# Layer 3's sum over states by accumulating transposes, gates laid out by tokens, softplus summed by transfers, and GpSimd's quarter of B in 14 of 16 states

## The chip, the cores and the metric

The kernel runs on one core of one Trainium2 chip. The metric is the device time of one execution in microseconds (us), as a median of several executions. Names used below: PE is TensorE (its weight loads are listed apart, as PEld), DVE is VectorE, ACT is ScalarE, POOL is GpSimd, SP is SyncE, which here only issues transfers.

## What is computed

Four residual layers are applied one after the other to x, of shape 4 x 256 x 64 x 64; each layer first normalizes x over groups of 8 channels. Layer 0 is a deformable convolution, layer 1 attention over the 4096 pixels, layer 2 a second deformable operator. The change lies in layer 3, a selective state space layer (Mamba) over the L = 4096 pixels as tokens, with 512 inner channels and 16 states:

```python
xz = jnp.einsum('bld,ed->ble', xs, in_proj_w)
u, res = jnp.split(xz, 2, axis=-1)
u_t = lax.conv_general_dilated(u_t, conv_w, ...)          # causal, 4 taps, each channel alone
u = jax.nn.silu(u_t.transpose(0, 2, 1) + conv_b)
dbc = jnp.einsum('bld,ed->ble', u, x_proj_w)
dt, Bm, Cm = jnp.split(dbc, [DT_RANK, DT_RANK + D_STATE], axis=-1)
delta = jax.nn.softplus(jnp.einsum('blr,dr->bld', dt, dt_proj_w) + dt_proj_b)
deltaA = jnp.exp(jnp.einsum('bld,dn->bldn', delta, A))
deltaBu = jnp.einsum('bld,bln,bld->bldn', delta, Bm, u)
def step(state, inp):
    dA, dBu, c_t = inp
    state = dA * state + dBu
    y = jnp.einsum('bdn,bn->bd', state, c_t)
    return (state, y)
...
y = jnp.moveaxis(ys, 0, 1) + u * D
y = y * jax.nn.silu(res)
out = jnp.einsum('ble,de->bld', y, out_proj_w)
```

## The kernel before

The four images are worked off one after the other, each through layers 0 to 3. All arithmetic of layer 3 that matters here is in fp32.

Layer 3 cuts the 4096 tokens into 8 chunks of 512 (C = 512, chunks numbered j) and walks over 8 x 16 states s, with j = s // 16 and n = s % 16. Channels lie on the 128 partitions, in four blocks dc of 128; a tile of "128 x 2048" is four blocks of 512 tokens. One iteration of the main loop does, for one state:

- `product` on DVE (L1594): h = du x B, where du = delta x u and B comes as a row broadcast to all partitions by a matmul on PE (`state`, tile bn, L1579). In the states listed in `helped`, DVE does three of the four blocks and POOL does the fourth (`quarter`, tile hq, L1586) from a row bs that a transfer has broadcast.
- `scan(dc)`, four times: ACT makes da = exp(delta x A) for one block into one of two PSUM banks (L1675), and DVE runs the recurrence over the 512 tokens (L1677). With two banks, the exp of block dc can start only when the scan of block dc - 2 is done.
- POOL keeps the last column as the carry for the next chunk (L1697), and multiplies h by C, broadcast by a transfer into cn (L1700).
- PE adds h into y, two states later (`add`, L1557): for each block, a matmul with the identity as weights and h as 512 moving columns, accumulating in one PSUM bank per block. State 0 also adds D x u with a diagonal weight (L1556).

`helped` holds the states 14, 15 and 0 to 5 of each chunk, but not states 14 and 15 of chunk 0. The transfers of cn and bs are issued on SP two states ahead (`ahead`, L1570).

The order of everything on PE, ACT, DVE and POOL is the program's order. Around the states, other work is put by hand into slots (state, half): half 0 comes after the second scan, half 1 after the fourth, half 2 after POOL's multiply. `front(j)` prepares chunk j during chunk j - 1: its steps count from state 11 of chunk j - 2 (step 0 is five states before chunk j - 1; for chunk 1 two). They are: normalized x, four projections to `up` (L1293), the convolution as four matmuls a block (L1333), silu at step 7 (state 2), the shares dt, B, C (L1360), then softplus. Softplus is written as relu(z) + ln(1 + exp(-|z|)), where POOL adds the parts: ACT makes |z| in du and relu(z) in delta (L1381, L1382, states 4 and 5), then du = exp(-|z|) (L1414, step 11, state 6), w = 1 + du (L1418, state 7), du = 1 - w (L1423, second half of state 8), w = ln w (L1426, state 9). POOL adds du, du and w to delta (L1429, after states 6, 9 and 11; the two du terms, exp(-|z|) and 1 - w, add up to the rounding loss of w), and makes du = delta x u after state 13 (L1430). In chunk 0, where chunk 1 is prepared, the same steps lie in states 8 to 13. Three casts (L1395 to L1403) and two small subtractions on POOL (L1397, L1401) split B into bf16 parts in between.

The gate `res` of chunk j is projected like u, block by block (`gate`, in states 9 and 10), with in_proj's columns as weights and x as moving data, and copied by ACT into sres[:, dc, :]. After all 16 states of a chunk, in state 2 of the next one, `gated` multiplies the four banks of y with silu(res) on DVE (L1646), and `close` projects the result with out_proj and adds x (L1449, L1453; two output tiles ot, in states 6 and 8), copies it out by ACT (L1457) and stores it. All these side works on PE share one PSUM bank (`bank`), so the next one starts when ACT has emptied it. The last chunk has no next chunk to prepare; its slots hold the building of the next image's table for layer 0 (`table`), which also sends 8 large transfers at a time through SP's queue.

Of the kernel before, what the change touches and what calls it, by code (L numbers as in the profile page):

```python
# [9 lines left out]
F32 = mybir.dt.float32  # L10
# [3 lines left out]
ALU = mybir.AluOpType  # L14
AX = mybir.AxisListType

P = 128
# [11 lines left out]
DS = 16  # L29
# [34 lines left out]
class Net:  # L64
# [1064 lines left out]
    def layer3(self, x, out, nxt, early):  # L1129
# [7 lines left out]
        nc, tc = self.nc, self.tc  # L1137
        C = 512
        NC, LEAD = N // C, 5
        with (  # L1140
# [7 lines left out]
            win, cw, al, dd = (early[n] for n in ("win", "cw", "al", "d"))  # L1148
            cb, xpw, dtw, dtb, wo = self.loads(pa, "l3b")
# [3 lines left out]
            diag = pa.tile([P, 4, P], F32, tag="diag", name="diag")  # L1153
# [16 lines left out]
            def bank():  # L1170
                return self.psum.tile([P, C], F32, tag="ps", name="front")
# [5 lines left out]
            def first():  # L1177
# [99 lines left out]

                state(0)
                c["gates"] = [spare() for _ in range(4)]
                for dc, pg in enumerate(c["gates"]):  # L1280
                    project(pg, xn, 4 + dc)

            def project(j, dc, to):
                c = chunks[j]

                def pe():
                    c["b"] = bank()
                    for ct in range(2):
                        nc.tensor.matmul(
                            c["b"], win[:, ct, bass.ts(dc, P)], c["xn"][:, ct, :], start=(ct == 0), stop=(ct == 1)  # L1290
                        )

                return pe, lambda: nc.scalar.copy(to(), c["b"])  # L1293

            def gate(j, dc):
                def to():
                    if dc == 0:
                        chunks[j]["sres"] = pb.tile([P, 4, C], F32, tag="sres", name="sres")
                    return chunks[j]["sres"][:, dc, :]

                return project(j, 4 + dc, to)

            def gate_silu(j):
                sres = chunks[j]["sres"]
# [2 lines left out]
            def front(j):  # L1307
# [117 lines left out]
                put(*at["c"], None, over)  # L1425
                put(*at["ln"], None, lambda: nc.scalar.activation(c["w"], c["w"], AF.Ln))  # L1426

                for step, part in zip(at["sums"], ("du", "du", "w")):
                    put(step, 2, None, lambda part=part: nc.gpsimd.tensor_add(c["delta"], c["delta"], c[part]))  # L1429
                put(at["sums"][3], 2, None, lambda: nc.gpsimd.tensor_mul(c["du"], c["delta"], c["u"]))  # L1430

                for dc in range(4):
# [5 lines left out]
            def close(j):  # L1438

                c = chunks[j]  # L1440
                last = j == NC - 1
                todo = []

                def project(ot):
                    def pe():
                        c["b"] = pda.tile([P, C], F32, tag="da", name="out") if last else bank()
                        c["z", ot] = c["b"]
                        for dc in range(4):
                            nc.tensor.matmul(  # L1449
                                c["b"], wo[:, dc, bass.ts(ot, P)], c["sres"][:, dc, :], start=(dc == 0), stop=False  # L1450
                            )
# [8 lines left out]
                    return pe, rest  # L1460

                for ot in range(2):
                    todo.append((6 + 2 * ot, 1, *project(ot)))
                if j < NC - 2:
                    todo.append((10, -1, None, lambda: fetch(j)))

                    todo.append((2 + DS, 0, None, lambda: count(j)))
                return todo
# [82 lines left out]
            def add(j, n, h, half):  # L1551
                c = chunks[j]
                for dc in (2 * half, 2 * half + 1):
                    if n == 0:
                        c["ys", dc] = py.tile([P, C], F32, tag="y", name="y")
                        nc.tensor.matmul(c["ys", dc], diag[:, dc, :], c["u"][:, dc, :], start=True, stop=False)  # L1556
                    nc.tensor.matmul(c["ys", dc], self.ident, h[:, dc, :], start=False, stop=(n == DS - 1))  # L1557


            hs, helped = {}, [s for s in range(NC * DS) if s % DS in (14, 15, 0, 1, 2, 3, 4, 5) and s // 2 != 7]  # L1560

            def ahead(s):

# [76 lines left out]
                    filled = filled or pe is not None  # L1640
                    rest()

            def gated(j):
                c = chunks[j]
                for dc in range(4):
                    nc.vector.tensor_mul(c["sres"][:, dc, :], c["ys", dc], c["sres"][:, dc, :])  # L1646

            with tc.manual_schedule(
                engines={
# [195 lines left out]
```

## Time and profile before

| | us |
|---|---|
| median of 4 executions | 9455.42 (9452.51 to 9462.64) |
| the profiled execution's own time | 9472.06 |
| its span, first to last instruction | 9470.3 |
| layer 3 of image 0, in that span | about 1480 to 2414 |

Busy time of each engine in the whole span: PE 8248.3 (87%), weight loads 4377.5 (46%), DVE 7355.9 (78%), ACT 4945.6 (52%), POOL 6967.6 (74%). The four images look alike: the page's 40 slices repeat a pattern of ten, of which the last four are layer 3. The costliest groups of layer 3, over all four images:

| line, engine | what | count | busy us | mean ns |
|---|---|---|---|---|
| L1700 POOL | h x cn, 128 x 2048 | 508 | 2300.9 | 4529 |
| L1677 DVE | scan, 128 x 512, input h | 1800 | 2174.3 | 1264 |
| L1675 ACT | exp to da, 128 x 512 | 2048 | 1395.9 | 689 |
| L1557 PE | y by the identity, 512 columns | 4096 | 1924.5 | 603 |
| L1594 DVE | product, 1536 or 2048 elements | 512 | 1025.1 | 2002 |

How to read it: an fp32 matmul leaves two records in the trace (4096 records of L1557 for 2048 matmuls), and the durations of PE's records overlap, so starts are compared instead. In a timeline, each line gives the start, the time, the engine, the line and the operation, with its shape, and how many instructions were merged; in brackets stands the idle time before it and what ended it. DVE's idle time in image 0's layer 3 is mostly put down to ACT's da: 10.0 us in 8 waits between 1505 and 2360.

### The profile page before, as it was taken

The numbers are of one execution on the slowest core, as the hardware profiler recorded it, in microseconds if no ns is written. First come the engines' busy times: TensorE is split into PE (matmuls) and PEld (weight loads), VectorE is DVE, ScalarE is ACT, GpSimd is POOL, SyncE is SP. The second block draws the span as 40 slices with busy tenths as digits, with TensorE's granted clock in tenths as the row PEclk, the third lists the DMA queues.
The fourth block names the chain that finished last, engine by engine and source line by source line (L and its number), as shares of the span: only waits on it lengthen the run. The fifth ranks groups of instructions, "written<-read, shape, count | busy, mean of one in ns | idle before, by whom it ended". The sixth has DMA issues, their size and how long they took to land. (4 is left out here: it accounts for less than half of the span.)

```text
span 9470.3 us, 94901 instructions
## 1 busy us (share of the span) xinstructions
PE 8248.3 (87%) x31767; PEld 4377.5 (46%) x31767; DVE 7355.9 (78%) x8241; ACT 4945.6 (52%) x7653; POOL 6967.6 (74%) x4164
## 2 busy tenths in 40 slices
PE   5789888998778988899877898889987789889997
PEld 3643464443464346344346434634434643563443
DVE  5764498999676449899967645999996764589998
ACT  4743335666574333666657433366665743336664
POOL 4746687998574668799856466879985746788997
PEclk9999999999999999999998999999999999999999
DMA  8840012222783001122378300122237820111221
GB/s 287 319 152 1 26 54 60 65 67 85 269 318 126 1 29 55 58 68 64 102 264 320 111 1 32 52 63 64 66 114 274 320 86 1 37 56 54 63 63 52
DMA packets 409189, 1017.75 MB, mean 107 GB/s; under 512 B 38833, under 2 KB 106834, under 8 KB 406642
## 3 DMA queue, kind: packets, MB, share of 16 engines
q0 software_dynamic: 165888, 604.05, 17.8%
q1 hardware_dynamic: 242802, 407.54, 14.1%
q8 instruction: 253, 4.15, 0.2%
q14 instruction: 246, 2.02, 0.1%
HBM read 849.60 MB, written 88.10 MB: 99 GB/s over the span
## 5 line engine op out<-in xcount | busy, mean ns | idle before, releaser
L1700 POOL TENSOR_TENSOR h<-h,cn 128x2048 f32<-128x2048 f32 x508 | 2300.9, 4529 | 41.3 <-POOL carry L1697 0.6
L1677 DVE TENSOR_TENSOR_SCAN h<-da,carry,h 128x512 f32<-128x512 f32 x1800 | 2174.3, 1264 | 82.1 <-ACT da L1675 33.9
L1675 ACT ACTIVATE da<-delta,l3a 128x512 f32<-128x512 f32 x2048 | 1395.9, 689 | 1208.3 <-DVE h L1677 1204.6
L1557 PE MATMUL y<-h,ident 128*128 128x512 f32 x4096 | 1924.5, 603 | 14.5 <-POOL h L1700 14.4
L371 POOL DMA_INDIRECT g<-tab,idx x1152 | 1361.9, 1182 | 706.4 <-DVE r L380 274.3
L592 POOL TENSOR_TENSOR acc<-acc,e 128x1024 f32<-128x1024 f32 x480 | 1125.9, 2346 | 540.3 <-ACT e L588 518.7
L415 PE MATMUL pz<-cols,l0w 128*128 128x256 f32 x4608 | 1218.9, 411 | 187.0 <-ACT cols L404 63.6
L1557 PEld LDWEIGHTS y<-h,ident 128*128 128x128 f32 x4096 | 788.7, 194 | 1063.0 <-issue 975.9
L380 DVE SCALAR_TENSOR_TENSOR r<-g,wx,r 128x512 f32<-128x512 f32 x1152 | 858.2, 745 | 372.7 <-ACT r L379 252.2
L489 DVE TENSOR_REDUCE m<-pm 128x3 f32<-128x1536 f32 (+2 forms) x340 | 599.5, 1763 | 700.2 <-PE pm L479 700.2
L415 PEld LDWEIGHTS pz<-cols,l0w 128*128 128x128 f32 x4608 | 898.9, 206 | 355.5 <-DVE cols L404 91.3
L588 ACT ACTIVATE e<-sc 128x1024 f32<-128x1024 f32 x512 | 496.1, 1020 | 1029.6 <-PE sc L575 1029.5
L1594 DVE TENSOR_TENSOR h<-du,bn 128x2048 f32<-128x2048 f32 (+1 forms) x512 | 1025.1, 2002 | 4.0 <-PE bn L1579 3.9
L599 PE MATMUL cx<-e,v 128*128 128x512 f32 x2048 | 1001.1, 616 | 0.0
L379 ACT ACTIVATE r<-g,wx 128x512 f32<-128x512 f32 x1152 | 826.4, 717 | 235.1 <-DMA g<-tab,idx 196.7
L882 DVE TENSOR_TENSOR prod<-ring,A 128x1280 f32<-128x1280 f32 (+1 forms) x640 | 783.6, 1266 | 67.3 <-DMA ring<-ring 37.0
L908 PE MATMUL pacc<-ident,prod 128*128 128x128 f32 x4864 | 631.8, 284 | 153.9 <-POOL prod L897 115.2
L908 PEld LDWEIGHTS pacc<-ident,prod 128*128 128x128 f32 x4864 | 555.4, 145 | 217.7 <-POOL prod L897 135.3
L397 PE MATMUL pt<-ident,acc 128*128 128x128 f32 x2304 | 428.6, 294 | 245.2 <-DVE acc L388 163.1
L599 PEld LDWEIGHTS cx<-e,v 128*128 128x128 f32 x2048 | 352.5, 189 | 599.4 <-issue 596.9
L387 ACT ACTIVATE acc<-r,wy 128x256 f32<-128x256 f32 x1152 | 571.5, 496 | 28.6 <-DVE r L380 25.8
L388 DVE SCALAR_TENSOR_TENSOR acc<-r,wy,acc 128x256 f32<-128x256 f32 x1152 | 548.6, 477 | 2.0 <-ACT acc L387 2.0
(271 smaller groups left out, 11452.9 us busy)
## 6 DMA issues: line engine op xcount, KB each, us to landing
cn<-cd SPq DMA_DIRECT2D x512, 256.0 KB
bs<-cd SPq DMA_DIRECT2D x248, 256.0 KB
tab<-vtnext SPq DMA_DIRECT2D x96, 512.0 KB
ring<-ring SPq DMA_DIRECT2D x288, 126.0 KB
ring<-ring SPq DMA_DIRECT2D x288, 124.0 KB
g<-tab,idx POOLq DMA_INDIRECT x1152
tab<-vt SPq DMA_DIRECT2D x28, 640.0 KB
x<-in_x SPq DMA_DIRECT2D x64, 256.0 KB
```

What stands on the lines that cost most here:

```text
L371: nc.gpsimd.indirect_dma_start(out=g[:], out_offset=None, in_=tab[:, :], in_offset=bass.IndirectOffsetOnAxis(ap=idx[:, t, k : k + 1], axis=0),
L379: nc.scalar.mul(r, g[:, :, 0, :], wx[:, 0, t, k : k + 1])
L380: nc.vector.scalar_tensor_tensor(r, g[:, :, 1, :], wx[:, 1, t, k : k + 1], r, ALU.mult, ALU.add)
L415: nc.tensor.matmul(sums[m][:, ot, :256], wf[:, i, bass.ts(ot, P)], cols[m][:, i, :], start=(i == 0), stop=(i == 17),)
L592: nc.gpsimd.tensor_add(b["acc"], b["acc"], e)
L599: nc.tensor.matmul(blocks[qb]["cx"], v[:, 4 * (i + kt // 4 * 4) + kt % 4, :], e[:, bass.ts(i % 2, 512)], start=(kt == 0 and i == 0), stop= ...
L908: nc.tensor.matmul(d["pd"][:, ct, t, :], prod[:, x, t, bass.ts(ct, P)], self.ident, is_transpose=True, start=(wy == 0 and x == left[0] and ...
L1557: nc.tensor.matmul(c["ys", dc], self.ident, h[:, dc, :], start=False, stop=(n == DS - 1))
L1594: nc.vector.tensor_mul(h[:, :d, :], c["du"][:, :d, :], c.pop(("bn", n)).to_broadcast([P, d, C]))
L1675: nc.scalar.activation(da, c["delta"][:, dc, :], AF.Exp, scale=al[:, dc, n : n + 1])
L1677: nc.vector.tensor_tensor_scan(h[:, dc, :], da, hb, carry[:, dc, n : n + 1], ALU.mult, ALU.add)
L1700: nc.gpsimd.tensor_mul(h, h, cn.to_broadcast([P, 4, C]))
```

## The change

Four things are changed together, all in layer 3.

1. **The sum over states by transposes.** `add` no longer multiplies h with the identity as weights. For each block dc and each of four blocks tb of 128 tokens, h's 128 x 128 block becomes the weights and the identity the moving data, in transpose mode, accumulating. y is then laid out by tokens: four banks ys[tb], with 128 tokens on the partitions and 512 channels along the row. D x u is added the same way, as a plain matmul with u as weights.
2. **The gates by tokens, and y turned back.** The gates are projected with x as weights and in_proj's gate columns as moving data, so that sres lies by tokens too, and `gated` multiplies block by block of tokens. The projection out of the layer needs channels on the partitions, so `close` gets four new steps `back(tb)`: four transposes into the shared bank and an ACT copy into a tile gd, which takes over a free buffer of `up` or of u. The first output projection moves from state 6 to state 7.
3. **Softplus summed by transfers.** For chunks 2 to 7, POOL's three additions to delta become transfers with addition, issued on POOL's queue. Chunk 1 keeps the additions.
4. **The quarter in 14 states.** `helped` holds all states but 12 and 13 of each chunk, and not 14 and 15 of chunk 0.

```diff
                 c["gates"] = [spare() for _ in range(4)]
-                for dc, pg in enumerate(c["gates"]):
-                    project(pg, xn, 4 + dc)
+                for tb, pg in enumerate(c["gates"]):
+                    for ct in range(2):
+                        nc.tensor.matmul(
+                            pg, xn[:, ct, bass.ts(tb, P)], win[:, ct, C:], start=(ct == 0), stop=(ct == 1)
+                        )
...
-            def gate(j, dc):
...
-                return project(j, 4 + dc, to)
+            def gate(j, tb):
...
+                def pe():
+                    c["b"] = bank()
+                    for ct in range(2):
+                        nc.tensor.matmul(
+                            c["b"], c["xn"][:, ct, bass.ts(tb, P)], win[:, ct, C:], start=(ct == 0), stop=(ct == 1)
+                        )
...
+                def sum(part):
+                    if j == 1:
+                        nc.gpsimd.tensor_add(c["delta"], c["delta"], c[part])
+                    else:
+                        nc.gpsimd.dma_start(out=c["delta"], in_=c[part], accum_op=ALU.add)
+
                 for step, part in zip(at["sums"], ("du", "du", "w")):
-                    put(step, 2, None, lambda part=part: nc.gpsimd.tensor_add(c["delta"], c["delta"], c[part]))
+                    put(step, 2, None, lambda part=part: sum(part))
...
-                                c["b"], wo[:, dc, bass.ts(ot, P)], c["sres"][:, dc, :], start=(dc == 0), stop=False
+                                c["b"], wo[:, dc, bass.ts(ot, P)], c["gd"][:, dc, :], start=(dc == 0), stop=False
...
+                def back(tb):
+
+                    def pe():
+                        c["b"] = py.tile([P, C], F32, tag="y", name="back") if last else bank()
+                        for dc in range(4):
+                            nc.tensor.transpose(
+                                c["b"][:, bass.ts(dc, P)], c["sres"][:, tb, bass.ts(dc, P)], self.ident
+                            )
+
+                    def rest():
+                        if tb == 0:
+                            if j < NC - 2:
+                                c["gd"] = pa.tile([P, 4, C + 3], F32, tag="up", name="gd")[:, :, :C]
+                            else:
+                                c["gd"] = pb.tile([P, 4, C], F32, tag="u", name="gd")
+                        nc.scalar.copy(c["gd"][:, :, bass.ts(tb, P)], c["b"].rearrange("p (d t) -> p d t", d=4))
+
+                    return pe, rest
+
+                late = j == NC - 2
+                for tb in range(4):
+                    at = ((3, 0), (3, 1), (4, 0), (4, 1)) if late else ((3, 0), (6, 0), (6, 1), (7, 0))
+                    todo.append((*at[tb], *back(tb)))
                 for ot in range(2):
-                    todo.append((6 + 2 * ot, 1, *project(ot)))
+                    at = ((6, 1), (8, 1)) if late else ((7, 1), (8, 1))
+                    todo.append((*at[ot], *project(ot)))
...
                 for dc in (2 * half, 2 * half + 1):
-                    if n == 0:
-                        c["ys", dc] = py.tile([P, C], F32, tag="y", name="y")
-                        nc.tensor.matmul(c["ys", dc], diag[:, dc, :], c["u"][:, dc, :], start=True, stop=False)
-                    nc.tensor.matmul(c["ys", dc], self.ident, h[:, dc, :], start=False, stop=(n == DS - 1))
+                    for tb in range(4):
+                        if n == 0:
+                            if dc == 0:
+                                c["ys", tb] = py.tile([P, C], F32, tag="y", name="y")
+                            nc.tensor.matmul(
+                                c["ys", tb][:, bass.ts(dc, P)],
+                                c["u"][:, dc, bass.ts(tb, P)],
+                                diag[:, dc, :],
...
+                        nc.tensor.matmul(
+                            c["ys", tb][:, bass.ts(dc, P)],
+                            h[:, dc, bass.ts(tb, P)],
+                            self.ident,
+                            is_transpose=True,
+                            start=False,
+                            stop=(n == DS - 1 and dc == 3),
+                            skip_group_check=True,
+                        )
...
-            hs, helped = {}, [s for s in range(NC * DS) if s % DS in (14, 15, 0, 1, 2, 3, 4, 5) and s // 2 != 7]
+            hs, helped = {}, [s for s in range(NC * DS) if s % DS not in (12, 13) and s // 2 != 7]
...
-                for dc in range(4):
-                    nc.vector.tensor_mul(c["sres"][:, dc, :], c["ys", dc], c["sres"][:, dc, :])
+                for tb in blocks:
+                    nc.vector.tensor_mul(c["sres"][:, tb, :], c["ys", tb], c["sres"][:, tb, :])
```

More of the change, by code (lines that the diff above doesn't have):

```diff
@@ L1293, in project @@
                 return pe, lambda: nc.scalar.copy(to(), c["b"])
-            def gate(j, dc):
[L1296 to L1299, printed above, removed]
-                return project(j, 4 + dc, to)
+            def gate(j, tb):
+                c = chunks[j]
+                def pe():
[6 more added lines that the diff above has]
+                    if tb == 0:
+                        c["sres"] = pb.tile([P, 4, C], F32, tag="sres", name="sres")
+                    nc.scalar.copy(c["sres"][:, tb, :], c["b"])
+                return pe, rest
             def gate_silu(j):
@@ L1460, in project, with rest @@
                     return pe, rest
+                def back(tb):
[5 more added lines that the diff above has]
+                            )
+                    def rest():
+                        if tb == 0:
+                            if j < NC - 2:
[3 more added lines that the diff above has]
+                        nc.scalar.copy(c["gd"][:, :, bass.ts(tb, P)], c["b"].rearrange("p (d t) -> p d t", d=4))
+                    return pe, rest
+                late = j == NC - 2
+                for tb in range(4):
+                    at = ((3, 0), (3, 1), (4, 0), (4, 1)) if late else ((3, 0), (6, 0), (6, 1), (7, 0))
+                    todo.append((*at[tb], *back(tb)))
                 for ot in range(2):
-                    todo.append((6 + 2 * ot, 1, *project(ot)))
+                    at = ((6, 1), (8, 1)) if late else ((7, 1), (8, 1))
+                    todo.append((*at[ot], *project(ot)))
                 if j < NC - 2:
@@ L1553, in add @@
                 for dc in (2 * half, 2 * half + 1):
-                    if n == 0:
-                        c["ys", dc] = py.tile([P, C], F32, tag="y", name="y")
-                        nc.tensor.matmul(c["ys", dc], diag[:, dc, :], c["u"][:, dc, :], start=True, stop=False)
-                    nc.tensor.matmul(c["ys", dc], self.ident, h[:, dc, :], start=False, stop=(n == DS - 1))
-            hs, helped = {}, [s for s in range(NC * DS) if s % DS in (14, 15, 0, 1, 2, 3, 4, 5) and s // 2 != 7]
+                    for tb in range(4):
[6 more added lines that the diff above has]
+                                diag[:, dc, :],
+                                start=(dc == 0),
+                                stop=False,
+                                skip_group_check=True,
[7 more added lines that the diff above has]
+                            stop=(n == DS - 1 and dc == 3),
+                            skip_group_check=True,
+                        )
+            hs, helped = {}, [s for s in range(NC * DS) if s % DS not in (12, 13) and s // 2 != 7]
             def ahead(s):
@@ L1641, in empty, with gated @@
                     rest()
-            def gated(j):
+            def gated(j, blocks=range(4)):
                 c = chunks[j]
-                for dc in range(4):
-                    nc.vector.tensor_mul(c["sres"][:, dc, :], c["ys", dc], c["sres"][:, dc, :])
+                for tb in blocks:
+                    nc.vector.tensor_mul(c["sres"][:, tb, :], c["ys", tb], c["sres"][:, tb, :])
             with tc.manual_schedule(
```

## The prediction

> **What bounds the kernel now.** I read the page's busy times first, then stretches of layer 3, then its groups, then one chunk of 16 states engine by engine. The page's totals name no single bound (PE 87%, DVE 78%, POOL 74%), so the layer that changes has to be read alone. Two stretches of 200 us inside image 0's layer 3, and one of layer 2 for later use (columns: length, busy PE, PEld, DVE, ACT, POOL, granted clock, DMA share, GB/s):
>
> ```profile
> 1150.00:1300.00 150.00, 131.60 (x806) 100.92 (x806) 141.12 (x175) 54.35 (x86) 133.10 (x104) 0.97 0.18 56
> 1600.00:1800.00 200.00, 189.13 (x448) 81.26 (x447) 197.04 (x153) 134.78 (x185) 186.41 (x86) 1.00 0.25 68
> 1800.00:2000.00 200.00, 191.03 (x452) 81.97 (x451) 197.50 (x156) 130.78 (x182) 187.64 (x87) 1.00 0.22 67
> ```
>
> DVE is busy 98.6%: it is the bound. POOL (94%) and PE (95%) stand close behind. PE's time can be checked: eight fp32 records of 512 columns span 3.60 us, so one starts every 0.43; some 420 of these and 28 of bn at 0.22 fill 187 of 200 us. What DVE does in a state with GpSimd's quarter and in one without:
>
> ```profile
> 1866.24 1.73 DVE L1594 TENSOR_TENSOR h<-du,bn 128x1536 f32<-128x1536 f32 x1
> 1868.07 3.63 DVE L1677 TENSOR_TENSOR_SCAN h<-da,carry,h 128x512 f32<-128x512 f32 x3
> 1871.62 1.26 DVE L1677 TENSOR_TENSOR_SCAN h<-da,carry,hq 128x512 f32<-128x512 f32 x1
> 1872.79 2.26 DVE L1594 TENSOR_TENSOR h<-du,bn 128x2048 f32<-128x2048 f32 x1
> 1875.16 4.81 DVE L1677 TENSOR_TENSOR_SCAN h<-da,carry,h 128x512 f32<-128x512 f32 x4
> 1879.88 2.26 DVE L1594 TENSOR_TENSOR h<-du,bn 128x2048 f32<-128x2048 f32 x1
> ```
>
> From product to product: 6.55 us with the quarter, 7.09 without. A chunk (state 14 at 1817.16 to the next at 1929.50) lasts 112.3. ACT in state 6 and POOL in state 7 of that chunk:
>
> ```profile
> 1873.55 0.61 ACT L1395 CAST bp<-dbc 64x512 bf16<-64x512 f32 x1
> 1874.17 0.61 ACT L1396 CAST bt<-dbc 64x512 bf16<-64x512 f32 x1
> 1874.81 1.91 ACT L1414 ACTIVATE du<-du 128x2048 f32<-128x2048 f32 x1
> 1876.63 0.67 ACT L1675 ACTIVATE da<-delta,l3a 128x512 f32<-128x512 f32 x1
> ...
> 1884.87 4.53 POOL L1429 TENSOR_TENSOR delta<-delta,du 128x2048 f32<-128x2048 f32 x1
> ```
>
> The exp that the third scan needs ends at 1877.30; that scan starts at 2.37 + 2.37 after the product, 1877.5. The spare is 0.2 us.
>
> **The sum, part by part** (four images; against the profiled execution's own 9472.06, which is its span 9470.3 and 1.8 around it; the median is 16.6 lower, and I carry the difference over to it).
>
> *Quarter in 14 states.* The list held 62 states of an image (8 x 8, less 14 and 15 of chunk 0); it will hold 110. 48 x 0.53 = 25.6 us, x4 = **-102**. In states 9, 10 and 11 of chunk 0 DVE already waits for ACT (0.21, 0.52, 0.93 us in its timeline), and a shorter product only lengthens these: +6.
>
> *Transposes for the sum.* Per state 8 records of 0.43 (3.44 us) become 16 of 128 columns. The nearest row is layer 2's own accumulating transpose, whose 16 take 1.97 us, one per 0.11:
>
> ```profile
> 1202.03 1.97 PE L908 MATMUL pacc<-ident,prod 128*128 128x128 f32 x16
> ```
>
> So 1.75 a state. Ends: 0.11 each, or 0.43 as for a 512-column record (6.9 a state, PE would bind); the row is the same form, I take 0.11. D's part, u as weights against 128 columns, becomes 32 records; 512 of L847 (256 columns) start every 0.2, so 6.4 us a chunk for 3.4. With 16 transposes back (1.8), 100 other records (43) and 16 bn (3.5) PE needs some 82 of 112 us. I give the 23 us that PE gains no worth, as DVE covers it; it buys slack.
> The Trainium skill, "TensorE: Matmul & The Clock Gate", Part 4 (PE-mode transpose), speaks against it: transposes don't count as busy and don't bring the full clock. At half clock these 82 would be 164 us a chunk, over +1000 us in all; but layer 2's stretch above, mostly transposes by count, was granted 0.97, and the row decides.
>
> *Turned back.* Per chunk four PE groups and four ACT copies (0.58, start to start 0.55, as L1293's). Where they fall:
> State 6, first half: the copy joins two casts and the exp of 1.8. Third scan wanted at 1.83 + 2.37 = 4.20 after the product; its exp now ends at 4.51 + 0.55 = 5.06. DVE waits 0.88. Chunks 1 to 6 have it: x24 = **+21**.
> State 7, second half: ot=0's projection now comes behind bn(8) (released by the product, 1.8) and the fourth copy: PE 2.0 to 6.3, copy at 6.5, two casts, next exp done at 8.9; wanted at 6.55 + 1.83 = 8.4. About 0.65 x24 = **+16**.
> State 3's copy fits before the third exp. Chunk 7's are spread singly: nothing.
>
> *Softplus by transfers.* POOL loses three adds of 4.53 in chunks 1 to 6 and gains three issues and 6 quarters of 1.24. The issue is not in the trace: 0.32 (SP's of L1570) below, 4.33 (the longest L371) above; L371's median 0.95, also on POOL, is nearest: 1.0. POOL's chunk: 14 x 5.97 (start to start of L1700 with a quarter) + 2 x 4.75 + du 4.53 + two subtractions 2.3 + 0.4 = 100.4, plus 3.0; DVE's: 14 x 6.55 + 2 x 7.09 + gating and statistics 3.6 = 109.6. POOL stays behind and costs nothing up to 3 us an issue.
> The first sum reads du, and L1423 (slot 8,1) overwrites du, so ACT now waits for the landing; behind it stand the next state's exps, and DVE. POOL: h x cn of state 6 starts 0.3 after the scans' end, 4.5, issue 1.0: off at +5.85. L1423 is due 6.55 + 6.5 = 13.1 after the same end. The flight F may take **7.25 us**. Bounds: the gather of 512 KB is first used 3.3 us after its issue ends (114.55 to 117.87); POOL's queue moved 604 MB in 17.8% of the span, 358 GB/s, so 1.46 of the 3.3 is data and 1.85 fixed. 1 MB moved once: 4.8. Both operands read: 1.85 + 5.86 = 7.7. Three passes, stretched by a quarter for the 0.25 DMA share: 12.9. I take 7.7, since the add has two operands: 0.45 x 24 = **+11**; ends 0 and +135.
> "DMA: Bandwidth & Descriptors", Bandwidth (measured), gives 6.15 us of engine time for a plain 1 MB on this path; doubled, an estimate, F is 14 and the whole becomes +119. The same table would put the gather near 5 where 3.3 is measured, so I keep the row.
> The later sums have more room: the second before the third 12 us, du's product two states.
>
> *Chunk 0* keeps POOL's adds, but hq(10) now stands before the subtraction for which the casts of state 10 wait (0.93 already): +1.25 x4 = **+5**. du for chunk 1 comes at 51.6 after state 8's scans, DVE wants it at 52.7: free, by 1 us.
>
> *Tail.* After the gating, 4 transposes and a copy more before the projection, which could start after the first of four gatings: +1.6 x4 = **+6**. 48 more loads of bs an image (0.32 each on SP): only state 11 of chunk 7 comes behind table writes (8 issues, some 13 us); it still lands before hq(11); nothing, a few us if not. Gates by tokens: the same records.
>
> Sum: -102 + 6 + 21 + 16 + 11 + 5 + 6 = **-37**: 9435 for a profiled execution, **9418** for the median.
>
> **Rivals.**
> A, slower: *the landing replaces the adds as a wait.* Without it the sum is -48, so each us of F over 7.25 gives back 24. From F = 10.0 the kernel is slower by 0.2%; at 11.5 it is +54 (9509), at 12.9 +87 (9542). For: the operation is unseen, and SP's broadcasts share the engines. Against: 358 GB/s were moved on this queue, and L3's DMA share is only 0.25.
> B, slower: *the issue is long.* At 4.33 POOL's chunk is 113.4 against 112.3 now, and POOL binds: +25, less 13 in chunk 7, and +11 of chunk 0 and tail: about 9478. It decides from 3.9 an issue, where POOL passes DVE with its waits. Against: 0.95 in 1152 issues' median.
> C: *no collisions.* ACT's slack is larger than I work out and F under 7.25: -102 + 6 + 5 + 6 = -85, 9370. Against: the 0.2 us spare in state 6.
> D: *balance.* F between 8.5 and 10: -18 to +19.
> E: PE at a lower clock, its projections late for ACT; the price is above.
> That the change doesn't do its part has little room: what it takes off DVE is plain in the rows.
>
> **How the numbers follow.** 0.2% (19 us) is about what a measurement here can tell from no change. Forecast (F under 8.5): 0.33, its own range 9390 to 9437. C 0.12, D 0.17, A 0.28, B 0.07, E and the unforeseen 0.03. Faster 0.33 + 0.12 = 0.45, same 0.17, slower 0.38. The range of 8 in 10 takes in C and A's upper end: 9360 to 9550.
>
> **What would show it.** Products of 1536 elements 440 times, of 2048 72 times; 6.55 us a state outside 6 to 9. DVE idle behind "ACT da" near 0.9 in state 6, 0.65 in state 7, and at state 9 behind an ACT that waits for a DMA; that wait is F less 7.25. Transposes of the sum at 0.11, clock near 1.0. L1429 down from 84 to 12. The prediction is wrong if POOL's DMA rows exceed 3 us, if DVE waits for hq, or if the chunk falls below 107 or above 113 us.

## The result and the profile after

| | before | changed |
|---|---|---|
| median, us | 9457.07 (9427.32 to 9469.52, 55 runs) | 9471.85 (9452.05 to 9492.91, 34 runs) |
| ratio, 95% interval | | 1.0017, 1.0012 to 1.0022 |
| span of the profiled execution | 9470.3 | 9483.2 |
| layer 3, first to last product, four images | 3601.6 | 3605.9 |
| of it VectorE idle (gaps over 0.15) | 40.1 | 146.4 |
| of it VectorE at work | 3561.5 | 3459.5 |
| last product to the next image's first normalization, images 0 to 2 | 77.6 | 103.6 |

The change made the kernel 0.17% slower, 16 us, where 37 fewer were forecast; that is still within the 0.2% that the prediction counts as no change. The lower half of the table comes from the starts and ends of VectorE's instructions: its work fell by 102 us and its idle time rose by 106; the ends of images 0 to 2 (called tails below, from the start of the last product) became 26 us longer. Together that is 30 us more. The same stretches of layer 3 as before (length, busy PE, PEld, DVE, ACT, POOL, granted clock, DMA share, GB/s):

```profile
1600.00:1800.00 200.00, 157.96 (x742) 100.26 (x741) 188.36 (x151) 136.96 (x190) 182.91 (x97) 0.95 0.39 103
1800.00:2000.00 200.00, 155.72 (x736) 100.05 (x736) 190.30 (x153) 130.15 (x184) 178.16 (x96) 0.94 0.39 102
```

DVE went from 197 us in 200 to 189, PE from 190 to 157, and PE's granted clock from 1.00 to 0.94. No engine is full any more. The page's group of scans names what DVE waits for, 145.5 us of ACT's exponentials where it was 33.9, and its group of hq shows a wait for bs that was not there:

```profile
L1737 DVE TENSOR_TENSOR_SCAN h<-da,carry,h 128x512 f32<-128x512 f32 x1608 | 1953.2, 1266 | 185.1 <-ACT da L1735 145.5
...
L1646 POOL TENSOR_TENSOR hq<-du,bs 128x512 f32<-128x512 f32 x440 | 575.6, 1309 | 63.6 <-DMA bs<-cd 42.8
```

DVE's idle time by the state in which it falls, from the first to the last product, summed over four images:

| state | 4 | 6 | 8 | 9 | 10 | others |
|---|---|---|---|---|---|---|
| before | 9.4 | 14.4 | 0 | 1.3 | 2.5 | 12.5 |
| changed | 37.7 | 32.3 | 20.5 | 29.4 | 12.8 | 13.7 |

*States 6 to 9.* In the timelines, DVE's products and scans of states 6 and 7 (start, time, engine, line; in brackets the idle time before and what ended it):

```profile
1877.40 1.73 DVE L1654 TENSOR_TENSOR h<-du,bn 128x1536 f32<-128x1536 f32 x1
1879.23 2.46 DVE L1737 TENSOR_TENSOR_SCAN h<-da,carry,h 128x512 f32<-128x512 f32 x2
1882.44 1.28 DVE L1737 TENSOR_TENSOR_SCAN h<-da,carry,h 128x512 f32<-128x512 f32 x1 [0.75 <-ACT da L1735]
1883.64 1.26 DVE L1737 TENSOR_TENSOR_SCAN h<-da,carry,hq 128x512 f32<-128x512 f32 x1
1884.82 1.73 DVE L1654 TENSOR_TENSOR h<-du,bn 128x1536 f32<-128x1536 f32 x1
```

ACT's state 6, and its du = 1 - w at the end of state 8:

```profile
1878.16 0.59 ACT L1496 COPY gd<-front 128x512 f32<-128x512 f32 x1
1878.64 0.62 ACT L1408 CAST bp<-dbc 64x512 bf16<-64x512 f32 x1
1879.27 0.62 ACT L1409 CAST bt<-dbc 64x512 bf16<-64x512 f32 x1
1879.91 1.91 ACT L1427 ACTIVATE du<-du 128x2048 f32<-128x2048 f32 x1
1881.73 1.28 ACT L1735 ACTIVATE da<-delta,l3a 128x512 f32<-128x512 f32 x2
...
1897.34 0.59 ACT L1476 COPY x<-front 128x512 f32<-128x512 f32 x1 [0.25 <-PE front L1472]
1898.80 2.01 ACT L1436 ACTIVATE du<-w,ones 128x2048 f32<-128x2048 f32 x1 [0.87 <-DMA delta<-du]
```

POOL's issue of the transfer that this waits for:

```profile
1889.81 0.85 POOL L1445 DMA_DIRECT2D delta<-du  x1
```

The copy, two casts and the exponential stand in front of the third scan's exp, and DVE waits 0.75 us. The issue ended at 1890.66 and its transfer had landed at 1898.80, 8.1 us later.

*State 4*, which costs most, begins on PE with what the prediction gave no wait: block 0 of y turned back, then the shares (L1373) in the same bank. The shares in one chunk of the kernel before:

```profile
1965.08 3.60 PE L1360 MATMUL front<-u,l3b 128*128 128x512 f32 x8
```

PE's timeline in the changed kernel:

```profile
1969.37 0.38 PE L1639 MATMUL bn<-bp,pickn 128*128 128x512 bf16 x1
1972.76 6.61 PE L1373 MATMUL front<-u,l3b 128*128 128x512 f32 x8 [3.01 <-ACT gd L1496]
```

The busy times and the clock (seventh column of figures) of these 8 us:

```profile
1972.00:1976.00 4.00, 3.24 (x4) 1.51 (x5) 4.00 (x4) 2.05 (x4) 4.00 (x1) 0.50 0.00 0
1976.00:1980.00 4.00, 4.00 (x13) 1.94 (x11) 1.80 (x2) 0.59 (x2) 3.92 (x4) 0.67 0.48 114
```

ACT, waiting for the shares:

```profile
1979.41 0.59 ACT L1377 COPY dbc<-front 128x512 f32<-128x512 f32 x1 [4.87 <-DMA cn<-cd]
1979.89 1.31 ACT L1735 ACTIVATE da<-delta,l3a 128x512 f32<-128x512 f32 x2
```

DVE, waiting for ACT:

```profile
1976.08 1.72 DVE L1654 TENSOR_TENSOR h<-du,bn 128x1536 f32<-128x1536 f32 x1
1980.62 3.75 DVE L1737 TENSOR_TENSOR_SCAN h<-da,carry,h 128x512 f32<-128x512 f32 x3 [2.82 <-ACT da L1735]
```

PE stands 3.01 us until ACT has emptied the bank; its clock is then 0.50, and eight records that took 3.60 before take 6.61. The copy of dbc, and state 4's first two exps behind it, come late; DVE waits 2.82. (The trace blames a transfer for ACT's 4.87; that copy reads only the shares.) Over all 24 chunks in which both stand there, the shares' time follows PE's gap: gaps up to 1.54 us, 3.7 us (8 chunks); 1.88 to 2.74, 5.2 to 5.4 (11); 2.87 and more, 6.6 to 6.8 (5). DVE's wait is that time less 3.8. (The 6.1 us that are left of state 4's 37.7 lie in chunk 0, and so did the 9.4 before.)

*The tail.* POOL's timeline in states 10 and 14 of image 0's last chunk, where it makes hq for the next state:

```profile
2378.12 1.26 POOL L1646 TENSOR_TENSOR hq<-du,bs 128x512 f32<-128x512 f32 x1 [5.89 <-DMA bs<-cd]
...
2408.33 1.26 POOL L1646 TENSOR_TENSOR hq<-du,bs 128x512 f32<-128x512 f32 x1 [8.57 <-DMA bs<-cd]
```

The last issues on SP's queue before the second of them:

```profile
2388.46 12.04 SPq L1576 DMA_DIRECT2D tab<-vtnext  x8
2400.60 1.45 SPq L1630 DMA_DIRECT2D cn<-cd  x1
2402.09 1.09 SPq L1630 DMA_DIRECT2D bs<-cd  x1
```

The row of state 15 is issued behind eight table writes, at 2402, and hq waits 8.57 us for it. In the kernel before, the two buffers of bs were free from state 5 on, and that hq did not wait:

```profile
2391.02 1.28 POOL L1586 TENSOR_TENSOR hq<-du,bs 128x512 f32<-128x512 f32 x1
```

The 5.89 us before the first hq, that for state 11, were POOL's alone: DVE did not wait in state 11 of this chunk. The 8.57 us reached DVE: its last scan, behind the last product and so in the tail, stood 2.82 us for this hq.

### The profile page after: what moved, and what is told of

It reads as the page before. It is cut to its first block, busy times and chain, and to the rows that moved or that the text cites. A ratio compares the mean times of both kernels' runs of the same rounds, so it can differ in the third digit from the quotient of the medians.

```text
span 9483.2 us, 106404 instructions
## 1 busy us (share of the span) xinstructions
PE 7731.8 (82%) x37143; PEld 4779.2 (50%) x37143; DVE 7260.3 (77%) x8241; ACT 5010.5 (53%) x7781; POOL 6968.8 (73%) x4356
## 5 line engine op out<-in xcount | busy, mean ns | idle before, releaser
L1737 DVE TENSOR_TENSOR_SCAN h<-da,carry,h 128x512 f32<-128x512 f32 x1608 | 1953.2, 1266 | 185.1 <-ACT da L1735 145.5
L371 POOL DMA_INDIRECT g<-tab,idx x1152 | 1385.0, 1202 | 665.3 <-issue 232.5
L1609 PEld LDWEIGHTS y<-ident,h 128*128 128x128 f32 x8192 | 1065.9, 154 | 459.9 <-issue 328.0
L1609 PE MATMUL y<-ident,h 128*128 128x128 f32 x8192 | 1221.1, 293 | 54.7 <-POOL h L1760 53.4
L1654 DVE TENSOR_TENSOR h<-du,bn 128x1536 f32<-128x1536 f32 (+1 forms) x512 | 922.5, 1802 | 0.0
L1646 POOL TENSOR_TENSOR hq<-du,bs 128x512 f32<-128x512 f32 x440 | 575.6, 1309 | 63.6 <-DMA bs<-cd 42.8
```

Of the source, the lines that this page charges most:

```text
L371: nc.gpsimd.indirect_dma_start(out=g[:], out_offset=None, in_=tab[:, :], in_offset=bass.IndirectOffsetOnAxis(ap=idx[:, t, k : k + 1], axis=0),
L1609: nc.tensor.matmul(c["ys", tb][:, bass.ts(dc, P)], h[:, dc, bass.ts(tb, P)], self.ident, is_transpose=True, start=False, stop=(n == DS - 1 ...
L1654: nc.vector.tensor_mul(h[:, :d, :], c["du"][:, :d, :], c.pop(("bn", n)).to_broadcast([P, d, C]))
L1737: nc.vector.tensor_tensor_scan(h[:, dc, :], da, hb, carry[:, dc, n : n + 1], ALU.mult, ALU.add)
```

## The experiments

Each kernel was timed beside the kernel before on its own chip (medians of before: 9249.5 beside the first four, 9498.7 the next four, 9449.9 the third four, 9495.8 the last two), so ratios are compared. "Layer 3" is the trace's first to last product plus the tails, against before; idle and tail are the quantities of the first table.

| kernel | ratio, 95% interval | layer 3, us | idle | tail |
|---|---|---|---|---|
| changed | 1.0017, 1.0012 to 1.0022 | +30 | 146.4 | 103.6 |
| e1 | 1.0006, 0.9998 to 1.0015 | 0 | 112.2 | 108.0 |
| e2 | 1.0001, 0.9992 to 1.0009 | +1 | 111.3 | 105.1 |
| e3 | 1.0006, 0.9994 to 1.0017 | +11 | 139.0 | 82.7 |
| e4 | 0.9988, 0.9980 to 0.9997 | -12 | 110.4 | 83.1 |
| e5 | 0.9979, 0.9970 to 0.9988 | -19 | 98.9 | 82.7 |
| e6 | 0.9956, 0.9942 to 0.9969 | -31 | 91.4 | 82.6 |
| e7 | 1.0030, 1.0019 to 1.0040 | +35 | 146.6 | 103.7 |
| e8 | 1.0048, 1.0035 to 1.0062 | +38 | 72.9 | 82.7 |
| f1 | 0.9953, 0.9939 to 0.9966 | -52 | 72.7 | 83.8 |
| f2 | 0.9946, 0.9930 to 0.9961 | -48 | 70.8 | 75.0 |
| f3 | 0.9995, 0.9986 to 1.0003 | -2 | 113.4 | 104.5 |
| f4 | 1.0019, 1.0010 to 1.0027 | +15 | 50.8 | 83.3 |
| g1 | 0.9973, 0.9963 to 0.9982 | -15 | 114.6 | 84.5 |
| g2 | 0.9908, 0.9892 to 0.9924 | -74 | 57.1 | 76.4 |

The trace's sum gives each ratio within 0.0015 (14 us), so most of what the kernels differ by lies in layer 3; differences under 14 us can't be read from one trace.

**e1: block 0 turned back earlier.**

```diff
-at = ((3, 0), (3, 1), (4, 0), (4, 1)) if late else ((3, 0), (6, 0), (6, 1), (7, 0))
+at = ((3, 0), (3, 1), (4, 0), (4, 1)) if late else ((2, 1), (6, 0), (6, 1), (7, 0))
```

> The changed kernel, with the first block of y turned back in the second half of state 2 instead of the first half of state 3 (chunks 1 to 6), so that its copy has freed the one PSUM bank before the shares of B, C and dt want it. VectorE's idle time before scans of state 4 was 12.2, 11.1, 10.9 and 3.5 us in the four images of the changed kernel, against 3.0, 1.8, 1.6 and 3.0 before. Theory (the bank is held by the copy, TensorE stands 2.7 to 3.0 us and comes back at a lower clock, so the copy of dbc on ScalarE and the exponentials behind it are late): the shares' 8 records take 3.6 us again, not 5.2 to 6.6, state 4's waits fall to at most 3 us an image, and the time falls by 20 to 30 us from 9472 to 9442 to 9452, under the kernel before. Rival (TensorE's clock is lower because transposes take the place of matmuls, wherever they stand): the shares stay over 5 us and state 4 keeps 10 us an image; time within 5 us of 9472. Rival (the wait is only moved): as much idle time in states 2 and 3 as state 4 loses; time within 5 us of 9472.

The shares took 3.6 to 3.7 us in all 24 chunks and state 4's idle time fell from 37.7 to 3.2 us. Layer 3 in the trace lost 30 us, as expected; the ratio fell by 0.0011, some 10 us and at most half of what was expected. State 8 took 10 us of it back, which e4 and e6 explain.

**e2: du = 1 - w later.**

```diff
-at = dict(e=(11, 0), w=(12, 0), c=(13, 1), ln=(14, 1), s=((11, 0), (12, 1), (15, 0)), sums=(11, 14, 16, 18))
+at = dict(e=(11, 0), w=(12, 0), c=(14, 0), ln=(14, 1), s=((11, 0), (12, 1), (15, 0)), sums=(11, 14, 16, 18))
```

> The changed kernel, with ScalarE's du = 1 - w half a state later (from the second half of state 8 to the first half of state 9). Theory (it waits there for the landing of the first accumulating transfer, 8.1 us after the end of its issue, 0.9 us too long, and the exponentials behind it are late): state 9's idle time of VectorE, 8.6, 6.6, 7.3 and 6.9 us in the four images, falls to at most 2 us each, and the time falls by some 20 us from 9472 to about 9452. Rival (ScalarE is simply full in states 8 and 9, and any order of its work ends at the same time): the idle time moves to states 9 and 10 and the time stays within 5 us. Rival (the second transfer is then late, and the third and du behind it): new idle time at the state that first uses delta and du, 1 us a chunk, and the time rises by 10 to 20 us.

State 9 fell from 29.4 to 12.4 us (expected at most 8) and the ratio to 1.0001, 15 us less. No later sum came late. In this trace state 4 also cost 12 us less than in the changed kernel, which the edit did not aim at; there, the shares of one chunk took 3.7 us even behind a gap of 3.11.

**e3: fewer quarters in the last chunk.**

```diff
-if s % DS not in (12, 13) and s // 2 != 7]
+if s % DS not in (12, 13) and s // 2 != 7 and not 118 <= s < 124]
```

> The changed kernel, with GpSimd's quarter left out in states 6 to 11 of the last chunk, as before the change. Theory (with the quarter in these states the two buffers of B's rows for states 14 and 15 come free too late, and their loads lie on SP's queue behind the table writes of the next image): the time from the last product to the next image's first normalization falls from 35.2, 33.7 and 34.7 us to about 26, a gain of some 26 us; six products an image are 0.53 us longer, 13 us in all; so 9472 - 13 = about 9459 (9454 to 9464). Rival (the tail is long because VectorE comes to the end of the chunk earlier and the table writes and statistics set its end): the tail stays at 33 to 35 us and the time rises by 13 us to 9485.

The tail fell by 21 us, to between 27.5 and 27.6 us an image, and hq no longer waits for bs. The rival falls. What is left, 1.7 us an image more than before, is about what the prediction had put there for turning y back (1.6).

**e4: all three.**

> The three edits together: the first block turned back in state 2, du = 1 - w half a state later, no quarter in states 6 to 11 of the last chunk. If the three losses are separate, the gains add: 25 + 20 + 13 = 58 us, so about 9414 (9400 to 9425), 0.4% below the kernel before. If they hide one another (ScalarE full in states 3 to 9, so that what is saved in one state is waited for in the next), under half of it: 9445 or more.

The gains did not add: 0.9988. State 8 had risen from 20.5 to 38.9 us. There, in one chunk, PE with the first projection of `close`:

```profile
1946.91 0.58 PE L1639 MATMUL bn<-bp,pickn 128*128 128x512 bf16 x1 [1.38 <-DVE h L1654]
1947.29 5.95 PE L1468 MATMUL front<-gd,l3b 128*128 128x512 f32 x8
```

The granted clock was 0.50 from 1947 to 1952. In 7 of 24 chunks this projection took 5.9 to 6.0 us and state 8 waited 3.3 us; in the other 17 it took 3.6 to 3.7, and the wait was 0.7 to 1.1.

**e6: work added to TensorE.** e4, and

```diff
-nc.tensor.matmul(bn[:, 0, :], pick[:, s % DS, :], c["bp"], start=True, stop=True)
+for i in range(9 if s % DS == 7 and s < NC * DS - DS else 1):
+    nc.tensor.matmul(bn[:, 0, :], pick[:, s % DS, :], c["bp"], start=True, stop=True)
```

> e4 with work added and none taken away: B's row matmul for state 7, of 0.26 us, is issued nine times instead of once (each writes the same values), in chunks 0 to 6, so that TensorE does not stand still in state 6. In e4 the first projection of state 7 took 5.95 us where the granted clock was 0.50 just before it, and 3.7 us elsewhere; VectorE then waited 3.3 us in state 8 instead of 0.8 to 1.1. Theory (the gaps that the removed matmuls left bring TensorE's clock down, and the next long chain on it is late): with the gap filled the projection takes 3.6 to 3.8 us in every chunk, no wait in state 8 is over 1.3 us, and the time falls by 15 to 20 us against e4, to 0.997. Rival (the clock falls for another reason, load of the whole chip or the kind of matmul): the 5 to 6 us projections stay, and 2 us more work on TensorE in each chunk makes the time the same or up to 25 us longer (0.9988 to 1.0015).

The same place in the same chunk:

```profile
2000.01 0.38 PE L1640 MATMUL bn<-bp,pickn 128*128 128x512 bf16 x1 [1.48 <-DVE h L1655]
2000.22 3.60 PE L1468 MATMUL front<-gd,l3b 128*128 128x512 f32 x8
```

All 24 projections take 3.6 us, state 8 is back at 19.3 us, and the kernel is faster with more work, 0.9956. The gap of 1.4 us just before bn is still there; an earlier one, 2.72 us long and ended 3.4 us before the projection, has shrunk to 1.0.

**f3: the same in state 3, nothing moved.** The changed kernel, and

```diff
-nc.tensor.matmul(bn[:, 0, :], pick[:, s % DS, :], c["bp"], start=True, stop=True)
+for i in range(9 if s % DS == 4 and s > DS else 1):
+    nc.tensor.matmul(bn[:, 0, :], pick[:, s % DS, :], c["bp"], start=True, stop=True)
```

> The changed kernel with nothing moved, and B's row matmul for state 4 issued nine times instead of once in chunks 1 to 7, so that TensorE has work in state 3 between the first block turned back and the shares, while ScalarE's copy holds the bank. VectorE's wait in state 4 was the shares' duration less 3.8 us in every chunk (5.2 to 5.4 us: 1.4 to 1.6; 6.6 to 6.7 us: 2.8 to 2.9; 3.7 us: none). Theory (the loss in state 4 is the clock after the gap, not the wait for the bank itself): the shares take 3.6 to 3.8 us, state 4 falls from 12.2, 11.1, 10.9 and 3.5 us to at most 2 us an image, and the time falls by some 30 us, from 1.0017 to about 0.9985 of the kernel before. Rival (the bank's wait is the loss and the clock a companion): shares at 3.6 us but starting as late, state 4 unchanged within 3 us an image, 1.001 to 1.003.

The chunk shown above, of this kernel:

```profile
1963.26 2.10 PE L1640 MATMUL bn<-bp,pickn 128*128 128x512 bf16 x9
1966.79 3.70 PE L1373 MATMUL front<-u,l3b 128*128 128x512 f32 x8 [1.42 <-ACT gd L1496]
```

The shares still wait for the bank: in the same 15 of 24 chunks, this one among them, they start 6.6 us after state 3's product both here and in the changed kernel (2.9 to 3.1 in the kernel before). There they took 5.2 to 6.8 us; here they take 3.6 to 3.7, as in all 24. State 4 falls from 37.7 to 9.3 us, about its value before the change, and the kernel from 1.0017 to 0.9995 (0.9985 was expected). The bank makes the gap; the clock after the gap makes the loss.

**e5: ScalarE's crowd spread out.** e4, and

```diff
-s=((11, 0), (12, 1), (15, 0))
+s=((13, 0), (16, 0), (18, 0))
...
+if ot == 0 and not late and not last:
+    pe, rest = project(ot)
+    todo.append((7, 1, pe, lambda: None))
+    todo.append((8, 0, None, rest))
```

> The three edits of e4 and two more: the copy of the first output block (behind y's projection) goes half a state later than its matmuls, to the first half of state 8, and the five casts of B and C move from states 6, 7 and 10 to 8, 11 and 13. Theory (VectorE's idle time is ScalarE's work that stands in front of the exponentials in crowded states): in e4 state 6 costs 8.1, 8.4, 8.4 and 6.7 us an image and state 8 10.8, 9.9, 13.3 and 4.9 us; with the casts gone from state 6 and the copy no longer waited for, each falls to at most 3 us, some 45 us together, and the time falls from e4's 0.9988 of the kernel before to 0.993 to 0.995. Rival (ScalarE is full from state 6 to 13, and each microsecond comes back in a later state): 0.998 to 0.999.

Missed: 0.9979. States 6 and 8 fell as expected, from 31.7 to 13.4 and from 38.9 to 0.5, but state 9 rose from 12.7 to 58.6. The late copy keeps the one bank, the second projection starts late behind it, and its copy stands in front of state 9's exps.

**e7: the quarter and the transfers without the turning.** The kernel before, with the change's `sum`, and

```diff
-if s % DS in (14, 15, 0, 1, 2, 3, 4, 5) and s // 2 != 7]
+if s % DS not in (12, 13) and s // 2 != 7]
```

> The kernel before with two parts of the change alone: GpSimd's quarter in 14 states and the softplus sums by accumulating transfers. The sum over states stays with identity matmuls, and nothing is turned. Products: 192 of them 0.53 us shorter, -102 us. Waits: ScalarE's du = 1 - w at the landing of the first transfer, state 9, +6 us an image; the tail of images 0 to 2 with B's rows behind table writes, +8 us each. Theory (the change's other losses come from turning y back: state 4's shares behind the copy, state 6's and 8's extra copies and projections, TensorE's clock): none of these is seen, the clock stays 1.00, and the time is about -102 + 24 + 24 = -54 us, 0.994 to 0.996 of the kernel before. Rival (TensorE, 95 us of each 100 busy before with chunks of 112.4 us, so about 107 us of work a chunk, becomes the bound when VectorE's part shrinks to about 108): TensorE over 98% busy, VectorE waits for front matmuls in states 0 to 5, time 0.997 to 1.000.

Missed, in the wrong direction: 1.0030. The turning's losses in states 4 and 8 are not seen (10.7 and 0.5 us; state 6 still costs 22.6), but states 9 and 10 cost 94 us. ACT in one chunk:

```profile
1904.18 0.58 ACT L1463 COPY x<-front 128x512 f32<-128x512 f32 x1
1907.45 2.00 ACT L1423 ACTIVATE du<-w,ones 128x2048 f32<-128x2048 f32 x1 [2.69 <-DMA delta<-du]
```

Without the turning's delays ACT gets to this instruction 5.9 us after the issue's end, not 7.3, and the landing takes 8.6. The losses of the changed kernel hide one another.

**f2: e7 with the landing out of the way**, by e2's and e3's edits.

> e7 (the kernel before with the quarter in 14 states and the sums by transfers, nothing turned) with du = 1 - w half a state later and no quarter in states 6 to 11 of the last chunk. In e7 states 9 and 10 cost 27.6, 22.6, 26.9 and 16.9 us, and in one chunk looked at ScalarE stood 2.69 us before du = 1 - w for the landing of the transfer, with a copy, a gate's matmuls and two exponentials behind it. Theory (that landing is e7's main loss, and it is smaller in the changed kernel only because ScalarE gets there later): states 9 and 10 fall to at most 6 us an image, the tail to 26 to 28 us; 60 + 8 us, 1.0030 becomes 0.995 to 0.997. Rival (TensorE, 96 to 98% busy in e7 with identity matmuls, is the bound, and the landing hides behind it): the idle time moves to other states, 1.001 to 1.003.

0.9946, a little more than expected; states 9 and 10 fall from 94 to 21 us. PE is 96.7% busy and not the bound.

**e8 and f4: the turning alone.** f4 has e1's and e6's edits as well.

```diff
-if j == 1:
+if True:
     nc.gpsimd.tensor_add(c["delta"], c["delta"], c[part])
...
-if s % DS not in (12, 13) and s // 2 != 7]
+if s % DS in (14, 15, 0, 1, 2, 3, 4, 5) and s // 2 != 7]
```

> The changed kernel with the quarter back in 8 states and the sums as GpSimd's additions: the transposes, gates by tokens and y turned back alone. VectorE's work is that of the kernel before. Theory: TensorE falls to about 80% busy and its granted clock to 0.95; the shares take 5 to 6.7 us and state 4 costs 10 us an image (3 in the last); states 6 and 8 cost 2 to 4 us an image more than before for the copies and projections; state 9 costs nothing; the tail stays 26 us: +40 to +60 us, 1.004 to 1.006. Rival (the longer states of 6.9 to 7.1 us in 6 to 11 give ScalarE room for the copies, and only state 4 is lost): +25 to +30 us, 1.003. Rival (TensorE's clock makes no difference to the end): within 10 us of before.

1.0048. State 4 costs 19.1 us and state 8 23.6, 9.7 and 23.6 over before; state 6 2.5. The clock is 0.90 to 0.96 in four windows of 100 us.

> e8 (transposes, gates by tokens and y turned back alone) with block 0 turned in state 2 and the row matmul for state 7 issued nine times. In e8 state 4 cost 3.7, 8.3, 6.6 and 0.5 us and state 8 3.4, 8.4, 6.8 and 5.0 us, 0.28 us a chunk where the projection took 3.6 us and 1.97 where it took 5.1 to 5.3. Theory (turning costs time by TensorE's lowered clock and the one bank, not in itself): shares and projections take 3.6 us everywhere, both states cost at most 2.5 us an image, and 1.0048 becomes 1.001 to 1.002. Rival (more work of ScalarE for the copies is the cost): 1.004 to 1.005.

1.0019, as expected, but by only part of the mechanism: state 4 fell to 4.7, state 8 only to 18.5. Seven of 24 projections still took 5.1 to 5.3 us; six of these had the same 2.01 us gap before them, ended 0.2 us earlier, as the 17 that took 3.6. The length of the gap alone does not decide.

**f1 and g2: the best of each.** f1 is e6 with e5's casts (not its late copy) and the quarter in states 0 to 9 of the last chunk. g2 is its counterpart without the turning: the kernel before, with the change's `helped` (so cut) and `sum`, e2's edit and e5's casts.

```diff
-if s % DS not in (12, 13) and s // 2 != 7]
+if s % DS not in (12, 13) and s // 2 != 7 and s < 122]
```

> e6 (block 0 turned in state 2, du = 1 - w later, TensorE kept busy before state 7) with the casts of B and C in states 8, 11 and 13, and the quarter in states 0 to 9 of the last chunk and not in its states 10 to 15. Theory (what is left in e6 is ScalarE's casts in front of exponentials: state 6 costs 8.1, 8.5, 8.5 and 6.7 us an image and state 8 4.9): state 6 falls to at most 4 us an image and state 8 to at most 1, 37 us together, and two more quarters in the last chunk give 4 us; 0.9956 becomes 0.991 to 0.992 of the kernel before. Rival (the wait comes back in state 9, as it did in e5, 11 us an image): 0.995 to 0.996.

> f1 without the turning: the kernel before with the quarter in 14 states (0 to 9 of the last chunk), the sums by transfers, du = 1 - w half a state later and the casts of B and C in states 8, 11 and 13. Theory (the turning takes work from TensorE, which did not set the end, and gives nothing in time): as fast as f1's 0.9953 or faster, 0.993 to 0.9955, with TensorE at 96 to 97% and a clock of 1.00. Rival (with VectorE's part at 107 us a chunk, TensorE's identity matmuls of 107 us a chunk are the bound, and only turning lets the casts' move bring anything): no gain over f2's 0.9946, or slower, 0.995 to 0.998.

f1 is at 0.9953, not 0.991: state 6 fell to 14.5 and state 8 to nothing, but state 9 rose to 28.4, as the rival said. g2 is the fastest kernel of all, 0.9908. Its stretches:

```profile
1600.00:1800.00 200.00, 195.71 (x467) 84.97 (x466) 197.35 (x158) 136.48 (x186) 189.63 (x100) 1.00 0.41 103
1800.00:2000.00 200.00, 194.47 (x462) 83.78 (x461) 197.39 (x159) 134.00 (x185) 185.41 (x100) 1.00 0.40 104
```

PE is 97% busy at full clock, and DVE is back at 197 in 200. DVE's work is the same in f1 and g2 (3471 and 3472 us); f1 has 16 us more idle time and 7 more of tail. The turning gives no time here, and costs some: 22 us by the traces, about 43 by the ratios, which were taken in different groups.

**g1: the two terms alone.** The changed kernel with f3's matmuls and f1's list of quarters.

> The changed kernel with two of its losses taken out and nothing else touched: the row matmul for state 4 issued nine times (as in f3) and the quarter in states 0 to 9 of the last chunk, not in its states 10 to 15. Theory (the prediction's sum of -37 us left out two terms, state 4 with 28 us over the kernel before and the tail with 24 us, and the rest of it held): without the two, and with four quarters of the last chunk fewer (4 x 0.53 x 4 = 8.5 us), it is -37 + 8 = -29 us against the kernel before, 0.997 (0.996 to 0.998). Rival (a further term is missing, or one of the sum's is wrong by more than 10 us): 0.9985 or more.

0.9973, as expected (26 us less than before). The trace's layer 3 gives 15 us less, which is outside what was expected for the sum alone and fits the sum with the landing's excess counted as well (below).

## Why the prediction was wrong, by its steps

Right:
- VectorE's gain. 102 us of work gone for the 102 of the quarter.
- Transposes: 16 in 1.91 us against 1.75 a state. The issue on POOL: 0.84 to 1.00 us where 1.0 was taken. POOL did not bind; chunk 0's hq(10) cost 7.5 us for 5 (state 10 there: 2.3 to 2.5 us an image, 0.5 before).
- The collision in state 6: 0.75 us for 0.88 in the chunk shown, and +18 us for +21 in all. State 8: +20.5 us for +16 (by the prediction's own figures, 8.9 less 8.4, it would have been 0.5 a chunk and +12, not 0.65 and +16).
- The turning in the tail, 1.7 us an image for 1.6, as e3 shows.

Right in kind, wrong in size:
- The landing as a wait. The transfer was allowed 7.25 us, and ACT in the chunk above was ready 7.27 after the issue's end. The flight was mis-sized: 8.1 us (median of 24) for 7.7, so 0.87 us in that chunk where 0.45 stood (its other estimate, a flight of 14 us, was much too long, and by its own sum would give +114, not +119). State 9 became +28 for +11, of which e2 took back 17. ACT's 24 waits there sum to 21.6 us, where 11 stood, and DVE lost somewhat more behind them than ACT waited.

Failed:
- "State 3's copy fits before the third exp." It does; what was left out is the next user of the same bank. The shares wait for the copy on PE, and come back at half clock. State 4: +28 us, priced at nothing. f3 and e1 each remove it, and f3 shows that the clock, not the wait for the bank, makes the loss.
- Rival E, "PE at a lower clock, its projections late for ACT", shared a chance of 0.03 with the unforeseen, because layer 2's stretch, mostly transposes, showed a mean clock of 0.97. A mean over 150 us was the wrong row: after the change the mean is still 0.94, and what costs is the clock in the 4 us behind a gap, in front of a chain that ACT waits for. The prediction held PE's gain for slack. The identity matmuls had kept PE at 95 of 100 and its clock at 1.00; taking them away opened the gaps.
- "Only state 11 of chunk 7 comes behind table writes ... nothing, a few us if not." States 14 and 15 do as well, since states 10 and 11 now hold their two buffers. The tail: +26 us where +6 was summed for it. e3 removes 21 of it.

The sum of -37, with +28 for state 4, +20 more for the tail and +17 more for the landing, gives +28; the trace's layer 3 has +30, the ratio +16. In the profiled pair the untouched gather of layer 0 was 17.6 us shorter in the changed kernel, so one execution cannot settle the difference, and it stays open. For g1, with state 4 and the tail's excess taken out and four quarters fewer in each last chunk, the sum is -29, or -12 with the landing's excess: the ratio says -26 (-35 to -17), the trace -15.

That the time came out within the prediction's 0.2% of no change, to which it gave 0.17, is luck: its rival D asked for a flight of 8.5 to 10 us, the flight was 8.1, and losses in state 4 and in the tail that the sum left out did the rest. Two of the prediction's own signs of being wrong came: DVE waited for hq, and 16 of 18 chunks of images 0 to 2 (from state 14 to state 14, the last of each image left out) lasted 113.0 to 115.4 us.

The Trainium skill, "TensorE: Matmul & The Clock Gate", Part 1, says that the clock is halved by how busy the array was in a free-running window of about 3.4 us. The 0.50 of the windows, and f4's equal gaps with unequal clocks, agree with it. The rule in its "Why this matters for your kernels", to avoid gaps over some 3 us, is too wide for this kernel: the shares were slow behind gaps of 1.88 us and more, though in e2 once fast behind 3.11. Part 4 says that transposes don't count as busy in the same way, which would make the real gap longer than the trace's; no run here separates that.

## What to carry to other kernels

Work taken off an engine that doesn't bind can still cost time: look for the gaps it leaves, and for the long matmul chains right behind them that another engine waits for; a few repeated matmuls in the gap are a cheap test. When an instruction is put before another user of a single buffer, price what that user's next user waits for, not only whether the instruction itself fits. When more transfers share two buffers and one queue, look again at those that were early only because the buffers were free.

## What the runs showed of the hardware

- TensorE's granted clock can drop to half (0.50 in the windows above) behind short gaps. In the changed kernel's profile the shares were never slow behind gaps up to 1.54 us (8 chunks) and always behind gaps from 1.88 us on (16); but in e2 they were fast once behind 3.11 us, and f4's projections were slow in 6 of 23 cases behind equal gaps of 2.01 us. No run gives a length from which the clock is sure to drop.
- A transfer that adds 1 MB to 1 MB inside the core takes POOL 0.84 to 1.00 us to issue. ScalarE's write that waits for it started 7.9 to 8.3 us after the issue in 20 of 24 chunks of the changed kernel (9.5 at most), and 8.6 (median) in e7.
- Between the groups of runs the kernel before took 9249.5 to 9498.7 us. The profiles put most of it in layer 0's gather, which no kernel here changes: 414 to 430 us an image in the first group, 471 to 492 in the second. Why it differs was not tested.
